# The 512x512 projections of a four-layer float32 attention kernel as seven half-size block products

## The chip, the cores and the metric

The kernel runs on one core of a Trainium2 chip. The metric is device time in microseconds (us), the median of several executions. All executions told here count as fast: none was over 1.5% above the fastest of its kernel. Executions of one kernel differ by up to 0.3% (2642.78 to 2650.27 us for the changed one), and a part of that spread turns out to have a cause of its own (see the experiment with filled waits). The granted clock is TensorE's clock as the profile records it, as a share of full speed.

TensorE is the matmul engine (PE in the profile, PEld for its weight loads), VectorE is DVE, ScalarE is ACT, SyncE is SP. SP's queue issues nearly all transfers (q1 on the page: 94.94 of 100.44 MB in the changed kernel). PSUM is the memory that TensorE writes its products to; the kernel uses it in pieces of 128x512 float32, called banks here. One float32 matmul leaves two records in the profile (a projection's 32 matmuls are 64 records). Line numbers (L326) differ between kernels.

## The reference, cut to what matters

Four layers follow one another on `x` of shape (4, 512, 32, 32), all in float32: four images of 512 channels and 1024 tokens.

```python
# layer 0: 8 heads of 64, softmax attention, residual
qkv = (xs @ Wp.T + bp).reshape(B, s, N_HEADS, 3 * D_K)
...
out = res @ Wo.T + bo + xs
# layer 1: linear attention: softplus features of 64, gated values, residual
# layer 2: layer norm over channels, one head of 512, residual
xn = (xf - mu) * jax.lax.rsqrt(var + EPS) * norm_w
qkv = jnp.einsum('bnc,dc->bnd', xn, w_qkv) + b_qkv
...
# layer 3: group norm (32 groups), 4 heads of 128, residual
qkv = conv1x1(group_norm(x, norm_w, norm_b), qkv_w, qkv_b)
...
return x + conv1x1(out, proj_w, proj_b)
```

Every projection is a 512x512 matrix times an image of 512x1024. There are four of them (q, k, v, output) per image in layers 0 and 3, and two in layer 2, where the kernel multiplies pairs of matrices into one beforehand (`wqk`, `wvo`).

## The kernel before

Everything goes by tiles of 128 partitions. `NC` is 4 (chunks of 128 channels), `TB` is 512 (half the tokens), `QT` is 4. Two pools of PSUM tiles matter: `acc` (two tiles of one bank) and `sc` (two tiles of two banks). A projection is a loop over token halves and output tiles, and its evictions (copies out of PSUM) alternate between VectorE and ScalarE:

```python
    def product(ps, lhs, rhs, cs=range(NC)):
        for c in cs:
            nc.tensor.matmul(
                ps, lhsT=lhs(c), rhs=rhs(c), start=(c == 0), stop=(c == NC - 1)
            )
...
    def project_qkv(w, bias, xb, first=False):
        ...
                for o in range(2 * NC):                  # q and k, by channels
                    ps = acc_tile()
                    product(
                        ps, lambda c: w[o // NC][:, c, bass.ts(o % NC, P)], lambda c: x[:, c, :]
                    )
                    slot()
                    evict(o, (q, k)[o // NC][tb][:, o % NC, :], ps, col(bias, o))
            for t in range(QT):                          # v, by tokens
                ps = acc_tile()
                product(ps, lambda c: x[:, c, bass.ts(t, P)], lambda c: w[2][:, c, :])
                slot()
                evict(t, v[tb][:, t, :], ps)
```

Work that is not on TensorE's path is cut into steps by generators and slipped between matmuls: each `slot()` runs one step of the first generator in `background` (linear attention of the image before, layer norm or group norm of the next), and `finish()` runs what is left of them at once. So how early background work is done depends on how many slots the stage ahead of it has. This will matter.

```python
    def slot():
        for p in pending:
            p[0] -= 1
        while pending and pending[0][0] <= 0:
            pending.pop(0)[1]()
        while background:
            if next(background[0], "end") != "end":
                break
            background.pop(0)
```

The layer norm of layer 2 has six steps for each half of the tokens, 12 in all; the last two of a half take the reciprocal of the deviation and write the normalized half (L592 and L595 in the prediction's lines). Layer 2's attention has 10 slots: two between score steps, and one for each of the four output chunks of both token halves. So the last two steps of the second half are left to `finish()` and run beside the next image's first products.

## Time and profile before

| | before |
|---|---|
| median of 3 executions | 2717.1 us (2716.29 to 2717.92) |
| span of the profiled execution | 2715.5 us |
| busy: TensorE, VectorE, ScalarE | 99%, 45%, 22% |
| moved by DMA | 32.17 MB |

The prediction shows the lines that say what bounds this kernel: TensorE, throughout. What TensorE waits for is very little, as the view of waits shows (engine, line, what it waited for: us in total, times, longest):

```profile
PE sc L289 <- ACT ptt L296: 7.4, 7, 2.9
PE sc L207 <- DMA wq<-in_wqkv: 5.6, 1, 5.6
PE sc L207 <- DVE q L371: 4.8, 1, 4.8
```

The first is at starts of attentions, where scores wait for exponentials; the second is the kernel's very first load; the third is its last projection. The largest two groups of projection matmuls on the page (columns: line, engine, operation, output and inputs, shape, count; then busy us and mean ns of one; then idle time ahead of them) have none:

```profile
L207 PE MATMUL po<-q,wo 128*128 128x512 f32 x480 | 211.6, 594 | 0.0
L207 PE MATMUL acc<-wv,x 128*128 128x512 f32 x256 | 115.9, 597 | 0.0
```

VectorE's float32 additions (`tensor_tensor`), on whose durations the prediction's costs rest, take 1217 ns for 128x1024 (L304) and 685 and 686 for 128x512 (L306, L371).

**A measure used below.** Waits in this view are only those where an instruction was released by another engine. To count all lost time, I took all of TensorE's records in order of start, and from each start-to-start time subtracted the pace of that record's shape (0.4289 us for 512 columns on the whole array, 0.2155 for 256, 0.111 for 128, 0.2145 for 512 columns on half the array, 0.07 for anything else). The paces are near the steps of the traces of before and after, whose medians are 0.429, 0.216 and 0.109 us for the first three shapes, and 0.430 for two records on half the array; the 0.07 is an assumption. The sum I call the *excess*. In the kernel before it is 89.4 us. Its absolute value depends on the paces chosen; differences between kernels hardly do.

### The profile page before, as it was taken

How to read it: one execution, taken by the hardware profiler on the slowest of the kernel's cores; microseconds unless marked ns; L12 is line 12 of the kernel's file. 1: busy time of each engine (PE TensorE's matmuls, PEld its weight loads, DVE VectorE, ACT ScalarE, POOL GpSimd, SP SyncE). 2: the span in 40 equal slices, each digit the busy share in tenths (PEclk: the TensorE clock that was granted, in tenths of full speed). 3: DMA queues.
4: the chain of work that ended last, by engine and by line, in shares of the span. 5: the costliest groups of instructions: out<-in, count | busy, mean ns of one | idle time of the engine just before them, and what ended most of it. 6: DMA issues, size and time to landing. Idle time of an engine off the chain costs nothing.

```text
span 2715.5 us, 17950 instructions
## 1 busy us (share of the span) xinstructions
PE 2690.0 (99%) x7490; PEld 1112.6 (41%) x7490; DVE 1232.7 (45%) x1359; ACT 602.5 (22%) x677; POOL 2.1 (0%) x12
## 2 busy tenths in 40 slices
PE   9999999999999999999999999999999999999998
PEld 4333433343334233444444444444444444444443
DVE  1466366636763877316144161321641651353154
ACT  0332143214321532111111111002310310220120
POOL 0000000000000000000000000000000000000000
PEclk9999999999999999999999999999999999999999
DMA  5000000000000000000000010000000000000000
GB/s 209 1 1 1 0 1 1 0 1 1 0 0 16 1 16 31 0 0 1 0 0 0 1 62 0 0 1 0 0 27 4 0 16 16 1 16 16 0 1 32
DMA packets 15448, 32.17 MB, mean 12 GB/s; under 512 B 1409, under 2 KB 1921, under 8 KB 15361
## 3 DMA queue, kind: packets, MB, share of 16 engines
q1 hardware_dynamic: 13056, 26.77, 2.7%
q10 hardware_dynamic: 2304, 4.20, 0.4%
q8 instruction: 60, 0.98, 0.2%
q14 instruction: 28, 0.22, 0.0%
HBM read 22.58 MB, written 8.39 MB: 11 GB/s over the span
## 4 chain that ended last, share of the span: by engine, by line
PE 96%; DVE 2%; ACT 1%; issue 0%; DMA 0%; SPq 0%; DVEq 0%; ACTq 0%
PE acc L207 32%; PE sc L289 25%; PE acc L322 16%; PE acc L337 8%; PE po L207 8%; PE den L358 1%; PE sc L207 1%; PE z L441 1%; PE den L353 1%; PE wval L543 1%; PE kx L488 1%; PE xtr L479 1%; PE kv L207 1%; PE lnsum L571 0%; DVE sum L304 0%
## 5 line engine op out<-in xcount | busy, mean ns | idle before, releaser
L296 ACT ACTIVATE ptt<-sc 128x1024 f32<-128x1024 f32 x416 | 412.0, 1022 | 843.3 <-PE sc L289 748.4
L289 PE MATMUL sc<-q,k 64*128 64x512 f32 (+1 forms) x1536 | 486.9, 610 | 7.4 <-ACT ptt L296 7.4
L322 PE MATMUL acc<-ptt,v 128*64 128x512 f32 (+1 forms) x1536 | 476.6, 600 | 0.0
L304 DVE TENSOR_TENSOR sum<-sum,ptt 128x1024 f32<-128x1024 f32 x272 | 330.9, 1217 | 218.5 <-ACT ptt L296 207.7
L289 PEld LDWEIGHTS sc<-q,k 64*128 64x128 f32 (+1 forms) x1536 | 184.5, 187 | 292.2 <-issue 204.0
L360 DVE RECIPROCAL r<-den 128x512 f32<-128x512 f32 x72 | 241.6, 3356 | 121.4 <-PE den L358 119.9
L322 PEld LDWEIGHTS acc<-ptt,v 128*64 128x64 f32 (+1 forms) x1536 | 159.7, 154 | 292.6 <-issue 289.0
L337 PE MATMUL acc<-ptt,v 128*128 128x512 f32 x512 | 223.4, 592 | 0.0
L289 PE MATMUL sc<-q,ln 128*128 128x512 f32 x512 | 221.1, 592 | 0.0
L207 PE MATMUL po<-q,wo 128*128 128x512 f32 x480 | 211.6, 594 | 0.0
L300 DVE TENSOR_TENSOR sum<-ptt 128x1024 f32<-128x1024 f32 x72 | 87.8, 1219 | 172.6 <-ACT ptt L296 171.9
L337 PEld LDWEIGHTS acc<-ptt,v 128*128 128x128 f32 x512 | 97.2, 190 | 122.0 <-issue 121.3
L289 PEld LDWEIGHTS sc<-q,ln 128*128 128x128 f32 x512 | 97.2, 190 | 122.0 <-issue 122.0
L220 DVE COPY v<-acc 128x512 f32<-128x512 f32 x48 | 33.2, 692 | 243.0 <-PE acc L207 243.0
L207 PEld LDWEIGHTS po<-q,wo 128*128 128x128 f32 x480 | 90.4, 190 | 118.0 <-issue 115.7
L386 DVE SCALAR_TENSOR_TENSOR x<-po,cs,x 128x512 f32<-128x512 f32 x60 | 45.1, 751 | 176.8 <-PE po L207 176.8
L207 PE MATMUL acc<-wv,x 128*128 128x512 f32 x256 | 115.9, 597 | 0.0
L207 PE MATMUL acc<-wvo,ln 128*128 128x512 f32 x256 | 113.1, 594 | 0.0
L207 PE MATMUL acc<-ln,wqk 128*128 128x512 f32 x256 | 112.2, 593 | 0.0
L207 PE MATMUL acc<-gn,wq 128*128 128x512 f32 x256 | 111.7, 592 | 0.0
L207 PE MATMUL acc<-gn,wk 128*128 128x512 f32 x256 | 111.2, 592 | 0.0
L207 PE MATMUL acc<-wv,gn 128*128 128x512 f32 x256 | 111.2, 592 | 0.0
(147 smaller groups left out, 1703.4 us busy)
## 6 DMA issues: line engine op xcount, KB each, us to landing
x<-in_x SPq DMA_DIRECT2D x3, 2048.0 KB, 20.4
out<-x SPq DMA_DIRECT2D x16, 256.0 KB, 2.0
out<-x ACTq DMA_DIRECT2D x16, 256.0 KB, 2.0
wo<-in_wo SPq DMA_DIRECT2D x3, 1024.0 KB, 5.5
wv<-in_wqkv SPq DMA_DIRECT2D x2, 1024.0 KB, 6.7
x<-in_x SPq DMA_DIRECT2D x4, 256.0 KB, 4.9
wq<-in_wqkv SPq DMA_DIRECT2D x4, 256.0 KB, 5.1
wk<-in_wqkv SPq DMA_DIRECT2D x4, 256.0 KB, 5.6
```

What stands on the lines that cost most here:

```text
L207: nc.tensor.matmul(ps, lhsT=lhs(c), rhs=rhs(c), start=(c == 0), stop=(c == NC - 1))
L220: nc.vector.tensor_copy(dst, ps)
L289: nc.tensor.matmul(ps[:, half, :], lhsT=s.k[key // QT][p0:p1, c, bass.ts(key % QT, P)], rhs=s.q[qb][p0:p1, c, :], start=(n == 0), stop=(n ...
L296: nc.scalar.activation(pt, ps, AF.Exp, scale=s.scale)
L300: nc.vector.tensor_tensor(t, s.pts[i - 1], pt, ALU.add)
L304: nc.vector.tensor_tensor(t, t, pt, ALU.add)
L322: nc.tensor.matmul(ps[p0:p1, :], lhsT=s.v[key // QT][:, key % QT, g * P + p0 : g * P + p1], rhs=pt[:, half, :], start=(key == 0), stop=(ke ...
L337: nc.tensor.matmul(ps, lhsT=s.v[key // QT][:, key % QT, bass.ts(n, P)], rhs=parts[key // 2][:, key % 2, :], start=(key == 0), stop=(key == ...
L353: nc.tensor.matmul(ps[half * s.hd : (half + 1) * s.hd, :], lhsT=ones[:, : s.hd], rhs=t[:, half, :], start=True, stop=True,)
L358: nc.tensor.matmul(ps, lhsT=ones, rhs=t[:, 0, :], start=True, stop=True)
L360: nc.vector.reciprocal(r, ps)
L386: nc.vector.scalar_tensor_tensor(xv, ps, s.eb[:, o : o + 1], xv, ALU.add, ALU.add)
```

## The change

The intent: split weights, inputs and outputs into 2x2 blocks of half size and compute the product with seven block products in place of eight, at the price of additions: 4 for the weights, 4 for the inputs, 7 for the outputs. Weights no longer stay in SBUF: they and their sums (kept in DRAM) are loaded anew for each image. The output projection moves from the middle of the attention to behind the next image's q. The order of products within a call, and which PSUM bank each goes to, is the table `SEVEN`: the last four products accumulate on a bank that has already been read once.

```diff
+    SEVEN = [
+        (1, 0, "put", (0, 0)), (2, 1, "add", (0, 0)), (7, 2, "put", (1, 1)), (6, 0, "put", (1, 0)),
+        (4, 2, "add", (1, 0)), (5, 0, "add", (1, 1)), (3, 0, "put", (0, 1)),
+    ]
...
+    def right(xb, tiles, over=False):
+        b11, b21 = xb[0][:, :HC, :], xb[0][:, HC:, :]
+        b12, b22 = xb[1][:, :HC, :], xb[1][:, HC:, :]
...
+        tt(t3, b22, b12, ALU.subtract)
+        tt(t1, b12, b11, ALU.subtract)
+        tt(t2, b22, t1, ALU.subtract)
+        tt(t4, b21, t2, ALU.subtract)
+        return {1: b11, 2: b21, 3: b22, 4: t4, 5: t1, 6: t2, 7: t3}
...
+    def two_by_sevens(factors, n, put, add):
+        banks = []
+        for _ in range(2):
+            pair_of = sc_tile()
+            banks.append([acc_tile()[:, :n], pair_of[:, 0, :n], pair_of[:, 1, :n]])
+        for i, bank, do, block_of in SEVEN:
+            for which in range(2):
+                ps = banks[which][bank]
+                for j in range(HC):
+                    lhs, rhs = factors(which, i, j)
+                    first = i in (1, 2, 7)
+                    nc.tensor.matmul(
+                        ps, lhsT=lhs, rhs=rhs, start=first and j == 0, stop=(j == HC - 1),
+                        skip_group_check=not first,
+                    )
+                (put if do == "put" else add)(which, block_of, ps)
+            slot()
...
+    def project_qkv(loads, bias, xb, before):
+        x = right(xb, [pt_tile] * 4)
+        q = [block("q") for _ in range(NTB)]
+        channels_first(loads.take("q"), x, q, bias=lambda o: col(bias, o))
+        if before is not None:
+            loads.start("k")
+            project_out(before, loads.take("o"))
+            loads.start("v")
...
+        k = [block("k") for _ in range(NTB)]
+        channels_first(loads.take("k"), x, k, bias=lambda o: col(bias, NC + o))
+        v = [block("v") for _ in range(NTB)]
+        tokens_first(loads.take("v"), x, v)
+        return q, k, v
...
+    def prepare():
+        for part in "qkvo":
+            if part == "o":
+                w = load("wo", d["wo3"])
+            else:
+                w = load("w", d["wqkv3"], "qkv".index(part))
+            for _ in range(3):
+                yield
+            keep_sums(f"{part}3", w)
+            yield
+        eb3.append(column_sums(w, "bqkv3", 2, "bo3"))
+        loads.start("q", "k")
+        yield
...
         else:
-            wo3 = load("wo", d["wo3"])
-            w3 = [load(n, d["wqkv3"], i) for i, n in enumerate(("wq", "wk", "wv"))]
             start_norm(group_norm, 0, "gn0")
+            background.append(prepare())
         Attention(b, q, xn, v, 1, None, eb).run()
         finish()
```

`put` is an eviction on ScalarE, `add` an addition from PSUM into the output on VectorE. `prepare`, which makes the sums of layer 3's weights and starts its first loads, runs in the background of layer 2's last attention.

More of the change, by code (lines that the diff above doesn't have):

```diff
@@ L67, in conv_fast @@
     PSUM = bass.MemoryType.PSUM
+    dram = ctx.enter_context(tc.tile_pool(name="dram", bufs=1, space=bass.MemoryType.DRAM))
     ps_acc = ctx.enter_context(tc.tile_pool(name="ps_acc", bufs=2, space=PSUM))
@@ L113, in conv_fast @@
         nc.sync.dma_start(xs[b], xin[b])
-    wv1 = load("wv1", d["wv1"])
-    w1 = block("w1")
-    wqk1 = w1[:, 0, :].rearrange("p (c o) -> p c o", c=NC)
-    nc.sync.dma_start(wqk1, by_chunk(d["wqk1"]))
-    bv1 = w1[:, 1, :]
-    nc.sync.dma_start(bv1, d["bv1"].partition_broadcast(P))
     bqk1 = const.tile([P, 2], F32, name="bqk1")
@@ L220, in evict, with first_qkv @@
             nc.vector.tensor_copy(dst, ps)
-    def project_qkv(w, bias, xb, first=False):
+    def first_qkv(w, bias, xb):
         q, k, v = [], [], []
@@ L233, in project_qkv @@
             v.append(block("v"))
-            if first and tb == 0:
+            if tb == 0:
                 banks = [s[:, i, :] for s in (sc_tile(), sc_tile()) for i in range(2)]
@@ L259, in project_qkv, with weight_parts, weight_sums @@
         return q, k, v
+    SEVEN = [
+        (1, 0, "put", (0, 0)), (2, 1, "add", (0, 0)), (7, 2, "put", (1, 1)), (6, 0, "put", (1, 0)),
+        (4, 2, "add", (1, 0)), (5, 0, "add", (1, 1)), (3, 0, "put", (0, 1)),
+    ]
+    HC = NC // 2
+    HO = C // 2
+    def weight_parts(w):
+        return w.rearrange("p (h j) (m n) -> p h j m n", h=2, m=2)
+    def weight_sums(w, name):
+        t = block(name)
+        s = t.rearrange("p c t -> p (c t)").rearrange("p (i j n) -> p i j n", i=4, j=HC)
+        a = weight_parts(w)
+        tt = nc.vector.tensor_tensor
+        tt(s[:, 0], a[:, 0, :, 1, :], a[:, 1, :, 1, :], ALU.add)
+        tt(s[:, 1], s[:, 0], a[:, 0, :, 0, :], ALU.subtract)
+        tt(s[:, 2], a[:, 0, :, 0, :], a[:, 0, :, 1, :], ALU.subtract)
+        tt(s[:, 3], a[:, 1, :, 0, :], s[:, 1], ALU.subtract)
+        return t
@@ new lines, in left @@
+    def left(w, sums):
+        a = weight_parts(w)
+        s = sums.rearrange("p c t -> p (c t)").rearrange("p (i j n) -> p i j n", i=4, j=HC)
+        return {
+            1: a[:, 0, :, 0, :], 2: a[:, 1, :, 0, :], 4: a[:, 1, :, 1, :],
+            5: s[:, 0], 6: s[:, 1], 7: s[:, 2], 3: s[:, 3],
+        }
+    def right(xb, tiles, over=False):
+        b11, b21 = xb[0][:, :HC, :], xb[0][:, HC:, :]
+        b12, b22 = xb[1][:, :HC, :], xb[1][:, HC:, :]
+        tt = nc.vector.tensor_tensor
+        t3, t2, t4 = (tiles[i]() for i in range(3))
+        t1 = b12 if over else tiles[3]()
+        tt(t3, b22, b12, ALU.subtract)
[3 more added lines that the diff above has]
+        return {1: b11, 2: b21, 3: b22, 4: t4, 5: t1, 6: t2, 7: t3}
@@ new lines, in pt_tile @@
+    def pt_tile(name="ptt"):
+        return work.tile([P, 2, TB], F32, tag="pt", bufs=5, name=name)
+    def two_by_sevens(factors, n, put, add):
[15 more added lines that the diff above has]
+            slot()
@@ new lines, in channels_first, with factors, first, more @@
+    def channels_first(a, b, out, put=None, bias=None):
+        def factors(which, i, j):
+            return a[i][:, j, bass.ts(which, P)], b[i][:, j, :]
+        def first(which, at, ps):
+            o = 2 * at[0] + which
+            if bias is None:
+                nc.scalar.copy(out[at[1]][:, o, :], ps)
+            else:
+                nc.scalar.activation(out[at[1]][:, o, :], ps, AF.Identity, bias=bias(o))
+        def more(which, at, ps):
+            c = out[at[1]][:, 2 * at[0] + which, :]
+            nc.vector.tensor_tensor(c, ps, c, ALU.add)
+        two_by_sevens(factors, TB, put or first, more)
@@ new lines, in tokens_first, with factors, at_block, put @@
+    def tokens_first(a, b, out):
+        for t0 in range(0, QT, 2):
+            def factors(which, i, j):
+                return b[i][:, j, bass.ts(t0 + which, P)], a[i][:, j, :]
+            def at_block(which, at):
+                return out[at[1]][:, t0 + which, bass.ts(at[0], HO)]
+            def put(which, at, ps):
+                nc.scalar.copy(at_block(which, at), ps)
+            def add(which, at, ps):
+                c = at_block(which, at)
+                nc.vector.tensor_tensor(c, ps, c, ALU.add)
+            two_by_sevens(factors, HO, put, add)
@@ new lines, in conv_fast, with keep_sums, load_left, __init__ @@
+    sums_in_dram = {}
+    def keep_sums(key, w):
+        t = weight_sums(w, "wsum")
+        kept = dram.tile([P, NC, TB], F32, tag=key, name="kept")
+        nc.sync.dma_start(kept, t)
+        sums_in_dram[key] = kept
+    def load_left(key, src, part=0):
+        w = load("w", src, part)
+        s = block("ws")
+        nc.sync.dma_start(s, sums_in_dram[key])
+        return left(w, s)
+    class Loads:
+        def __init__(s, layer):
+            s.layer, s.ready = layer, {}
+        def start(s, *parts):
+            for part in parts:
+                if part == "o":
+                    s.ready[part] = load_left(f"o{s.layer}", d[f"wo{s.layer}"])
+                else:
+                    i = "qkv".index(part)
+                    s.ready[part] = load_left(f"{part}{s.layer}", d[f"wqkv{s.layer}"], i)
+        def take(s, part):
+            return s.ready.pop(part)
@@ new lines, in project_out, with put, add, factors @@
+    def project_out(att, a):
+        b = right(att.q, [lambda: pair("t3"), lambda: pair("t2"), pt_tile], over=True)
+        def put(which, at, ps):
+            o = 2 * at[0] + which
+            att.add_to_x(at[1], o, ps, done=(at == (0, 1)))
+        def add(which, at, ps):
+            o = 2 * at[0] + which
+            xv = xs[att.b][:, o, bass.ts(at[1], TB)]
+            nc.vector.tensor_tensor(xv, ps, xv, ALU.add)
+            att.store_x(at[1], o)
+        def factors(which, i, j):
+            return a[i][:, j, bass.ts(which, P)], b[i][:, j, :]
+        two_by_sevens(factors, TB, put, add)
@@ new lines, in project_qkv @@
+    def project_qkv(loads, bias, xb, before):
[6 more added lines that the diff above has]
+            loads.start("v")
+        else:
+            loads.start("v")
+        if before is not None and before.then is not None:
+            background.append(before.then())
+        k = [block("k") for _ in range(NTB)]
[3 more added lines that the diff above has]
+        return q, k, v
@@ L261, in conv_fast, with __init__ @@
     class Attention:
-        def __init__(s, b, q, k, v, heads, wo, eb, store=False, last=False):
+        def __init__(s, b, q, k, v, heads, wo, eb, store=False, last=False, then=None):
             s.b, s.q, s.k, s.v, s.wo, s.eb = b, q, k, v, wo, eb
-            s.store, s.last = store, last
+            s.store, s.last, s.then = store, last, then
             s.hd = C // heads
@@ L294, in scores @@
                     )
-            pt = work.tile([P, 2, TB], F32, tag="pt", bufs=5, name="ptt")
+            pt = pt_tile()
             nc.scalar.activation(pt, ps, AF.Exp, scale=s.scale)
@@ L371, in normalize @@
             nc.vector.tensor_tensor(s.q[qb][:, g, :], s.accs.pop((qb, g)), r, ALU.mult)
-            if g == s.groups - 1 and not (s.last and qb == NTB - 1):
+            if s.last and g == s.groups - 1 and qb < NTB - 1:
                 later(3, lambda: s.project_out(qb))
@@ L382, in out_product, with add_to_x, store_x @@
             product(ps, lambda c: s.wo[:, c, bass.ts(o, P)], lambda c: s.q[qb][:, c, :], cs)
-        def add_to_x(s, qb, o, ps):
+        def add_to_x(s, qb, o, ps, done=True):
             xv = xs[s.b][:, o, bass.ts(qb, TB)]
             nc.vector.scalar_tensor_tensor(xv, ps, s.eb[:, o : o + 1], xv, ALU.add, ALU.add)
+            if done:
+                s.store_x(qb, o)
+        def store_x(s, qb, o):
             if s.store:
-                (nc.scalar if o % 2 else nc.sync).dma_start(xout[s.b, :, o, bass.ts(qb, TB)], xv)
+                (nc.scalar if o % 2 else nc.sync).dma_start(
+                    xout[s.b, :, o, bass.ts(qb, TB)], xs[s.b][:, o, bass.ts(qb, TB)]
+                )
         def run(s):
@@ L651, in idle @@
             yield
-    eb = None
+    att = None
+    loads = Loads(0)
     for b in range(B):
         xb = [xs[b][:, :, bass.ts(tb, TB)] for tb in range(NTB)]
-        if b > 0:
-            background.append(idle(3))
-            background.append(linear_attention(b - 1))
-        q, k, v = project_qkv(w0, "bqkv0", xb, first=(b == 0))
         if b == 0:
+            for key, w in zip(("q0", "k0", "v0", "o0"), w0 + [wo]):
+                keep_sums(key, w)
+            q, k, v = first_qkv(w0, "bqkv0", xb)
             eb = column_sums(wo, "bqkv0", 2, "bo0")
+            wv1 = load("wv1", d["wv1"])
+            w1 = block("w1")
+            wqk1 = w1[:, 0, :].rearrange("p (c o) -> p c o", c=NC)
+            nc.sync.dma_start(wqk1, by_chunk(d["wqk1"]))
+            bv1 = w1[:, 1, :]
+            nc.sync.dma_start(bv1, d["bv1"].partition_broadcast(P))
+        else:
+            q, k, v = project_qkv(loads, "bqkv0", xb, att)
         if b == B - 1:
@@ L665, in conv_fast @@
             rawk = load("rawk", d["wraw2"], 1)
-        Attention(b, q, k, v, 8, wo, eb).run()
+            rawq = load("rawq", d["wraw2"], 0)
+        else:
+            loads.start("q", "o")
+        att = Attention(b, q, k, v, 8, None, eb, then=lambda b=b: linear_attention(b))
+        att.run()
+    loads.start("o")
     finish()
-    rawq = load("rawq", d["wraw2"], 0)
-    rawv = load("rawv", d["wraw2"], 2)
-    wo = load("wo", d["wo2"])
-    background.append(linear_attention(B - 1))
     def fold(lhs, rhs, name):
@@ L688, in conv_fast @@
     u = column_sums(rawk, "bqkv2", 0)
+    flush()
+    rawv = load("rawv", d["wraw2"], 2)
+    wo = load("wo", d["wo2"])
+    project_out(att, loads.take("o"))
+    background.append(att.then())
+    wqk = left(wqk, weight_sums(wqk, "wqks"))
     wvo = fold(rawv, wo, "wvo")
     eb = column_sums(wo, "bqkv2", 2, "bo2")
+    wvo = left(wvo, weight_sums(wvo, "wvos"))
+    loads = Loads(3)
+    eb3 = []
+    def prepare():
+        for part in "qkvo":
+            if part == "o":
+                w = load("wo", d["wo3"])
+            else:
+                w = load("w", d["wqkv3"], "qkv".index(part))
[6 more added lines that the diff above has]
+        yield
     for b in range(B):
         xn = norms.pop(f"ln{b}")
-        q, v = [], []
-        for tb in range(NTB):
-            q.append(block("q"))
-            v.append(block("v"))
-            for o in range(NC):
-                ps = acc_tile()
-                product(ps, lambda c: wqk[:, c, bass.ts(o, P)], lambda c: xn[tb][:, c, :])
-                slot()
-                evict(o, q[tb][:, o, :], ps, u[:, o : o + 1])
-            for t in range(QT):
-                ps = acc_tile()
-                product(ps, lambda c: xn[tb][:, c, bass.ts(t, P)], lambda c: wvo[:, c, :])
-                slot()
-                evict(t, v[tb][:, t, :], ps)
+        x = right(xn, [pt_tile] * 4)
+        q = [block("q") for _ in range(NTB)]
+        channels_first(wqk, x, q, bias=lambda o: u[:, o : o + 1])
+        v = [block("v") for _ in range(NTB)]
+        tokens_first(wvo, x, v)
         if b + 1 < B:
@@ L710, in conv_fast @@
         else:
-            wo3 = load("wo", d["wo3"])
-            w3 = [load(n, d["wqkv3"], i) for i, n in enumerate(("wq", "wk", "wv"))]
             start_norm(group_norm, 0, "gn0")
+            background.append(prepare())
         Attention(b, q, xn, v, 1, None, eb).run()
         finish()
-    eb = column_sums(wo3, "bqkv3", 2, "bo3")
+    att = None
     for b in range(B):
-        q, k, v = project_qkv(w3, "bqkv3", norms.pop(f"gn{b}"))
-        if b + 1 < B:
+        last = b == B - 1
+        q, k, v = project_qkv(loads, "bqkv3", norms.pop(f"gn{b}"), att)
+        if last:
+            wo = load("wo", d["wo3"])
+        else:
             start_norm(group_norm, b + 1, f"gn{b + 1}")
-        Attention(b, q, k, v, 4, wo3, eb, store=True, last=(b == B - 1)).run()
+            loads.start("q", "o")
+        att = Attention(b, q, k, v, 4, wo if last else None, eb3[0], store=True, last=last)
+        att.run()
         finish()
```

## The prediction

> **What bounds the kernel now.** I read the page's busy times first, then its slices, then the chain that ended last.
>
> ```profile
> span 2715.5 us, 17950 instructions
> PE 2690.0 (99%) x7490; PEld 1112.6 (41%) x7490; DVE 1232.7 (45%) x1359; ACT 602.5 (22%) x677; POOL 2.1 (0%) x12
> ...
> PE   9999999999999999999999999999999999999998
> ...
> DVE  1466366636763877316144161321641651353154
> ...
> PE 96%; DVE 2%; ACT 1%; issue 0%; DMA 0%; SPq 0%; DVEq 0%; ACTq 0%
> PE acc L207 32%; PE sc L289 25%; PE acc L322 16%; PE acc L337 8%; PE po L207 8%; PE den L358 1%; PE sc L207 1%; PE z L441 1%; PE den L353 1%; PE wval L543 1%; PE kx L488 1%; PE xtr L479 1%; PE kv L207 1%; PE lnsum L571 0%; DVE sum L304 0%
> ```
>
> TensorE is busy in every slice and is 96% of the chain. Line 207 is the helper that every 512x512 projection goes through, and holds 40% of the chain (acc and po). A busy PE need not be a PE at its pace, so I took the pace from the timeline of two projections of the last layer, and from a burst of narrow matmuls in layer 1:
>
> ```profile
> 2516.94 13.90 PE L207 MATMUL acc<-gn,wq 128*128 128x512 f32 x32
> 2530.68 13.90 PE L207 MATMUL acc<-gn,wk 128*128 128x512 f32 x32
> ...
> 311.97 1.05 PE L507 MATMUL kxt<-halves,kx 128*128 128x128 f32 x8
> ```
>
> From start to start, 32 records take 13.74 us: 0.4293 us each, with no gap. The program has half as many matmuls, so one float32 matmul is two records, 0.859 us for 512 columns. The narrow ones: the last of the 8 lasts 0.275 us (that line's median), so 7 steps take 0.775 us, 0.111 us each. A weight load is listed as 0.19 us there too, and yet the step is 0.111: loads overlap each other as well as matmuls. So matmuls of 256 columns, between the two, should run at half the 512-column step, near 0.216 us, and not be held by their weight loads.
>
> [...]
> - [...] Only multiplications with TensorE count here; the additions that replace them cost TensorE nothing.
> - [...] 1217 ns for 1024 elements (line 304), 685 to 690 for 512.
> - [...] bank 0 is read after products 1, 6, 5 and 3 and accumulated on in between. Only waits, no extra instructions; no part of the trace before does it.
>
> **What the change removes.** A projection of one image (512x512 weights by 1024 tokens) is now 4 x 4 x 2 = 32 matmuls, 64 records, 27.5 us. Seven half-size products are 7 x 2 output tiles x 2 chunks = 28 matmuls of 512 columns (56 records, 24.0 us), or, where tokens come first, 56 of 256 columns (112 records x 0.2158, about 24.2 us). The eighth that falls away is 8 x 0.4293 = 3.43 us.
>
> How many projections change, from the diff: layer 0 images 1 to 3 q, k, v and all four outputs, 13; layer 2 q and v of four images, 8; layer 3 q, k, v of four and the output of three, 15. In all 36 (25 by channels, 11 by tokens); the first image's q, k, v and the last output stay. So TensorE loses 36 x 3.43 = 123.6 us, and gets back 11 x 0.13 = 1.5 for halved columns.
>
> **What it adds.** On VectorE, all from the durations above:
> - Input sums: 4 subtractions of 128x1024, 4.9 us, for 11 inputs (q, k and v share one) and 7 outputs: 88 us.
> - Adds into C: 6 of 512 (0.69 us) per channel call, 12 of 256 (estimate 0.42, from the slope between 512 and 1024) per token call. Against the evictions that VectorE now makes (4 a projection, or 8 in an output), that is about +1.1 us for each of 18 q/k, +2.3 for 11 v, +4.1 for 7 outputs: 74 us.
> - Weight sums, 4 x 0.69 us for 10 matrices: 28 us.
>
> Together +190 us, so VectorE goes to about 1420 of 2600 us, 55%: off the path as a whole. ScalarE gets the plain evictions, +3 to 5 us a projection, and has room at 22%.
>
> Transfers: 28 loads of 2 MB (weights and sums) and 8 MB of sums written. The start of the trace moves about 400 GB/s and single 1 MB weight loads land in 5.0 to 7.8 us, so a pair needs some 11 us. q and o are loaded over a whole attention stage (110 us and more); k waits for old k and v blocks, but is used only two products later, 48 us; v gets q's blocks, 48 us before its use. Hidden.
>
> **What can come onto the path.** Four places.
>
> (a) Within a call, product 3 accumulates in the bank of product 5, and must wait for VectorE's add of 5. With two tiles interleaved there is one tile's product in between: 4 x 0.429 = 1.72 us. An eviction starts about 0.21 us after the next product does (VectorE's q eviction at 2520.58; the product that starts at 2516.94 ends 8 steps later, at 2520.37), takes 0.69, and TensorE starts about 0.11 us after a release (scores at 360.85 after an exponential that ends at 360.74): 1.0 of 1.72. By tokens it is 0.21 + 0.42 + 0.11 = 0.74 of 0.86. It fits, but any 1.2 us instruction ahead of the add on VectorE stalls TensorE up to 0.5 to 1.1 us. That happens where VectorE has other work: beside linear attention, and while the next sums are made. Estimate 1.5 us for each of the six handovers between images in layers 0 and 3, and 2 us for each of three linear attentions beside projections: 15 us.
>
> (b) Layer 2 is tighter, since seven-product order wants both token halves at once:
>
> ```profile
> 1625.09 13.90 PE L207 MATMUL acc<-ln,wqk 128*128 128x512 f32 x32
> ...
> 1626.01 3.35 DVE L592 RECIPROCAL rstd<-rstd 128x512 f32<-128x512 f32 x1
> ...
> 1629.85 2.73 DVE L595 SCALAR_TENSOR_TENSOR ln<-ln,cols,rstd 128x512 f32<-128x512 f32 x4
> ```
>
> The normalized second half is ready at 1632.6, 7.5 us after projections start; today it is first read 27 us after. Products 1 and 2 need only the first half and last 6.9 us; product 7 needs one subtraction more (1.2 us), at 8.7. So 1.9 us of stall, in three of four images: 6 us.
>
> (c) At a handover, both accumulators must be free before product 1 of the second tile, and the last group's is freed only after its denominators, 3.4 us reciprocal and multiplication: in layer 3 the last value matmul is through at 2460.9 and that multiplication at 2467.0. Product 1 of the first tile and product 2 of both (5.2 us) can go first. Under 1 us, counted in (a).
>
> (d) The first and the middle stage (sums of first weights, output of image 3 between two foldings, layer 3's sums made in the background): VectorE is idle from 24 to 31 us, DRAM traffic there ends at 40. Estimate 3 us.
>
> Sum: 2717.1 - 123.6 + 1.5 + 15 + 6 + 3 = 2619; I state 2617, since a schedule can move instructions past a stall.
>
> **Rivals.**
> 1. *VectorE takes over in layer 0.* In its attention it has 108 busy of 158 us (the stretch from 92 to 250), and without the output product in mid attention that stretch shrinks by 13.7 us for TensorE but only 3 for VectorE. If linear attention also slid there (it now starts two products later), it would exceed 85%. It has about 20 steps, and k and v offer 21 slots, so I think it still ends before. If not, some 10 us in each of three images: 2650.
> 2. *The bank chain stalls at every call*, because evictions are queued behind input sums: 47 two-tile calls (25 + 22) at 1 us would be 47 us: 2650. For it: slack by tokens is only 0.12 us. Against: VectorE has 8.0 busy of 67.9 us in layer 3's projections now (2035 to 2103).
> 3. *Narrow matmuls are bound by weight loads* at 0.3 us: 11 x 112 x 0.085 = 105 us more, 2720, the gain gone. The 0.111 us step speaks against it, though only in bursts of 8.
> 4. *No stalls:* 2717.1 - 122 = 2595.
>
> **Range and chances.** The removal is sure arithmetic; the uncertainty is all stalls, from nearly none (2597) to rivals 1 or 2 (2650). The 2% line lies at 2662.8, so stalls would have to reach 68 us. Faster by over 2%: 0.93; within: 0.06; slower: 0.01.
>
> **What would show it.** Right: PE busy near 2570, in the seven-product group 0.43 us a record of 512 columns and 0.216 of 256; idle of PE before these products, released by VectorE, 15 to 30 us in all; VectorE near 1420; no wait of PE on a load over 1 us after the start. Wrong: token products above 0.25 us a record; PE idle in layer 0's attention behind VectorE; a wait for sums from DRAM at the start of layer 3 or at k.

## The result, and the profile after

| | before | after |
|---|---|---|
| median | 2717.22 us (2716.29 to 2717.92, 4 runs) | 2649.31 us (2642.78 to 2650.27, 4 runs) |
| ratio | | 0.9745 (95%: 0.9728 to 0.9762): faster |
| span of the profiled execution | 2715.5 us | 2641.1 us |
| excess over pace | 89.4 us | 137.3 us |
| moved by DMA | 32.17 MB | 100.44 MB |

Ratios are the mean time of one kernel's fast runs over that of the other's in the same rounds, so not quite the ratio of the medians. The gain is 68 us where 100 were forecast. The time lies inside the stated range, at its very edge.

The page of the changed kernel, in the parts that the prediction shows of before (busy times, VectorE's slices, the chain that ended last):

```profile
span 2641.1 us, 19557 instructions
...
PE 2584.7 (98%) x7818; PEld 1174.1 (44%) x7818; DVE 1410.6 (53%) x1637; ACT 690.1 (26%) x881; POOL 2.1 (0%) x12
...
DVE  2486477646864887426345153252762563365254
...
PE 92%; DVE 4%; ACT 2%; issue 1%; DMA 0%; SPq 0%; DVEq 0%; ACTq 0%
PE sc L470 25%; PE acc L326 18%; PE acc L503 17%; PE sc L326 12%; PE acc L518 8%; PE acc L202 3%; PE den L539 1%; PE sc L202 1%; PE z L628 1%; PE den L534 1%; PE wval L730 1%; PE kx L675 1%; DVE sum L485 1%; PE xtr L666 1%; PE po L202 1%
```

TensorE lost 105 us of busy time and is still the bound. VectorE gained 178 us, to 1410.6, and has no slice above 8 tenths. But TensorE's share of the chain fell from 96% to 92%, and VectorE's doubled: some of the path now runs through VectorE. The projections are lines 326 (30% of the chain; the first image's and the folded ones are still line 202).

**The pace is as forecast.** The timeline of the last image's v in layer 3, by tokens (start us, duration us, engine, line, operation and count):

```profile
2464.49 1.89 PE L326 MATMUL acc<-ws,ptt 128*128 128x256 f32 x8
2466.22 1.89 PE L326 MATMUL sc<-w,ptt 128*128 128x256 f32 x8
2467.95 1.89 PE L326 MATMUL acc<-ws,ptt 128*128 128x256 f32 x8
```

Eight records take 1.73 us, 0.216 us each. In numbers for the whole: the span fell by 74.4 us and the excess rose by 47.9, so the work at pace fell by 122.3, against 123.6 - 1.5 = 122.1 in the prediction. The whole miss is in the excess.

**Where the excess came from.** The view of TensorE's waits, without the three lines that answer to those of before (7.1, 5.3 and 4.8 us) and the ones below 1.6 us:

```profile
PE sc L326 <- DVE ptt L303: 11.2, 3, 3.8
PE acc L326 <- DMA w<-in_wqkv: 7.5, 1, 7.5
...
PE sc L326 <- DVE q L348: 4.2, 3, 1.4
PE acc L326 <- ACT v L363: 3.4, 4, 0.9
PE sc L326 <- DVE v L367: 2.6, 3, 0.9
```

Two lines make 18.7 of these 28.9 us. The first is product 7 at the start of images 1 to 3 in layer 2. The timeline of the last of them:

```profile
1591.01 3.35 DVE L779 RECIPROCAL rstd<-rstd 128x512 f32<-128x512 f32 x1
...
1595.51 0.69 DVE L348 TENSOR_TENSOR q<-sc,q 128x512 f32<-128x512 f32 x1 [1.15 <-PE sc L326]
...
1596.12 2.73 DVE L782 SCALAR_TENSOR_TENSOR ln<-ln,cols,rstd 128x512 f32<-128x512 f32 x4
1598.76 0.68 DVE L348 TENSOR_TENSOR q<-sc,q 128x512 f32<-128x512 f32 x1
1599.36 1.22 DVE L303 TENSOR_TENSOR ptt<-ln 128x1024 f32<-128x1024 f32 x1
...
1600.64 3.70 PE L326 MATMUL sc<-ptt,wqks 128*128 128x512 f32 x8 [3.52 <-DVE ptt L303]
```

VectorE worked here in the order of its queue. After the reciprocal, which ends at 1594.36, it sits 1.15 us waiting for product 2 of the first tile, because that tile's add (1595.51) stands ahead of the normalization; then come the four normalizing instructions, then the second tile's add, and only then the difference `t3` (L303) that product 7 reads. The adds cost 1.4 us and the wait 1.15. TensorE, from the start-to-start times, loses 3.68 us here and 3.99 twice before.

The second line is layer 3's first weight load. VectorE and the DMA queue of SP, in the timeline of that start:

```profile
1752.91 1.20 SPq L100 DMA_DIRECT2D w<-in_wqkv  x1
...
1761.97 0.68 DVE L283 TENSOR_TENSOR wsum<-wo,wsum 128x512 f32<-128x512 f32 x1
1762.55 2.05 PE L326 MATMUL acc<-gn,w 128*128 128x512 f32 x2 [7.51 <-DMA w<-in_wqkv]
...
1762.68 0.34 SPq L377 DMA_DIRECT2D kept<-wsum  x1
1763.12 0.38 SPq L383 DMA_DIRECT2D ws<-kept  x1
```

The load of q's weights was issued at 1752.91, 2 us before TensorE wanted them, and TensorE ran on at 1762.55. The sums (`ws`) were loaded later still: they stand in SP's queue behind the store of the output matrix's sums, which were finished at 1762.65. `prepare` needs 17 slots and comes after group norm, which takes 8 of the attention's 10. So most of `prepare` is run by `finish()`, at the end, all at once.

The smaller lines are in layer 0. The handover of images, at q of image 1:

```profile
222.40 3.35 DVE L541 RECIPROCAL r<-den 128x512 f32<-128x512 f32 x1
...
225.67 0.63 DVE L348 TENSOR_TENSOR q<-sc,q 128x512 f32<-128x512 f32 x1
...
226.35 1.98 PE L326 MATMUL sc<-ptt,ws 128*128 128x512 f32 x4 [1.38 <-DVE q L348]
```

The add of product 2 stands behind a reciprocal of the last attention's denominators, and product 7 of the same tile starts only after the add. It costs 1.55 us of TensorE's time in each of three images. The `v` lines are evictions that stand behind linear attention's softplus, on ScalarE (1.10 us, three times) and on VectorE (1.04, three times). Last, there are steps that are 0.07 to 0.15 us too long, 0.10 on average: between two records of one shape they are 124 in this kernel and 72 before. The recorded texts call them restarts after a wait, but the profile records a release within 0.3 us before only 23 of the 124 and 4 of the 72, so what delays the others is not shown.

### The profile page after: what moved, and what is told of

Same layout as the page of the kernel before. It is cut to its first block, busy times and chain, and to the rows that moved or that the text cites. A ratio compares the mean times of both kernels' runs of the same rounds, so it can differ in the third digit from the quotient of the medians.

```text
span 2641.1 us, 19557 instructions
## 1 busy us (share of the span) xinstructions
PE 2584.7 (98%) x7818; PEld 1174.1 (44%) x7818; DVE 1410.6 (53%) x1637; ACT 690.1 (26%) x881; POOL 2.1 (0%) x12
## 2 busy tenths in 40 slices
DMA packets 35953, 100.44 MB, mean 38 GB/s; under 512 B 2448, under 2 KB 2960, under 8 KB 31248
## 4 chain that ended last, share of the span: by engine, by line
PE 92%; DVE 4%; ACT 2%; issue 1%; DMA 0%; SPq 0%; DVEq 0%; ACTq 0%
PE sc L470 25%; PE acc L326 18%; PE acc L503 17%; PE sc L326 12%; PE acc L518 8%; PE acc L202 3%; PE den L539 1%; PE sc L202 1%; PE z L628 1%; PE den L534 1%; PE wval L730 1%; PE kx L675 1%; DVE sum L485 1%; PE xtr L666 1%; PE po L202 1%
## 5 line engine op out<-in xcount | busy, mean ns | idle before, releaser
L367 DVE TENSOR_TENSOR v<-sc,v 128x256 f32<-128x256 f32 x88 | 37.3, 424 | 144.8 <-PE sc L326 143.1
L326 PE MATMUL acc<-ptt,ws 128*128 128x512 f32 x224 | 102.5, 595 | 0.0
L363 ACT COPY v<-acc 128x256 f32<-128x256 f32 x132 | 48.7, 372 | 148.1 <-PE acc L326 148.1
L344 ACT ACTIVATE k<-acc,cols 128x512 f32<-128x512 f32 x42 | 28.9, 687 | 215.2 <-PE acc L326 215.2
L567 DVE SCALAR_TENSOR_TENSOR x<-acc,cs,x 128x512 f32<-128x512 f32 x74 | 55.4, 749 | 51.9 <-PE acc L326 51.3
L326 PE MATMUL sc<-ptt,w 128*128 128x512 f32 x168 | 76.6, 594 | 0.0
L344 ACT ACTIVATE q<-acc,cols 128x512 f32<-128x512 f32 x42 | 28.9, 687 | 175.7 <-PE acc L326 175.7
L326 PEld LDWEIGHTS acc<-ptt,ws 128*128 128x128 f32 x224 | 42.1, 190 | 55.2 <-issue 50.7
L348 DVE TENSOR_TENSOR q<-sc,q 128x512 f32<-128x512 f32 x44 | 29.9, 679 | 68.1 <-PE sc L326 68.1
L348 DVE TENSOR_TENSOR k<-sc,k 128x512 f32<-128x512 f32 x28 | 19.4, 691 | 81.4 <-PE sc L326 81.4
```

The lines of the kernel that those rows point to most:

```text
L326: nc.tensor.matmul(ps, lhsT=lhs, rhs=rhs, start=first and j == 0, stop=(j == HC - 1), skip_group_check=not first,)
L344: nc.scalar.activation(out[at[1]][:, o, :], ps, AF.Identity, bias=bias(o))
L348: nc.vector.tensor_tensor(c, ps, c, ALU.add)
L567: nc.vector.scalar_tensor_tensor(xv, ps, s.eb[:, o : o + 1], xv, ALU.add, ALU.add)
```

## The experiments

Twelve runs, all correct. The first four ran on one chip and the other eight on a second; the kernel before took 2717.85 us in the first round, and 2717.55 and 2716.84 in the two on the second chip. The main theory: the missing 32 us are the two long waits, and both come from how early background work is done, not from the seven products. The rival: they come from the call's own structure (chain of banks, two-bank tiles, narrow token products). The two moves below settle the 30 us that they win; the 24 us of excess over the kernel before that they leave stay with the rival, in part open.

**after_again**, the changed kernel unchanged, as a measure.

> The changed kernel again, as the measure for the other three. In its profile TensorE loses 48 us more in steps longer than their pace than the kernel before does. Theory A (named waits): 13.5 us of it at the starts of three images of layer 2, 10.6 us at the start of layer 3, the rest in layer 0 and in restarts of 0.1 us. After each wait of some 4 us TensorE runs steps of 0.85 in place of 0.43 us in some executions and not in others, which is why executions differ: expect 2642 to 2651, clock 0.991 to 0.995. Rival B (the loss is spread over all 47 two-tile calls): the same time, but the same loss of about 1 us in every call.

Measured: 2649.2 us (2648.55 to 2649.33), 0.9746 of before's 2717.85. The excess of this profiled execution is 143.1 us, so the 2642.78 of the first was a lucky one (137.3).

**norm_early.** Layer 2's layer norm gets more slots, so that it is through before the next image starts:

```diff
                 s.add_to_x(qb, n, ps)
                 slot()
+                if s.b + 1 < B:
+                    slot()
...
-                if not s.one or i % s.per:
+                if not s.one or i % s.per or s.b + 1 < B:
                     slot()
```

> The layer norm of the next image runs two steps where it ran one in layer 2's attention, so it is done before the projections start. Theory A: the three waits of product 7 for its input sum (3.99, 3.99 and 3.68 us) go, and the slow steps after them: 12 to 17 us less than the changed kernel of the same round, clock up by 0.002 to 0.003. Rival B: at most 4 us less. Rival C (VectorE is too full in layer 2, the earlier norm only moves the wait into the attention): TensorE waits in layer 2's attention instead, under 4 us gained.

Measured: 2633.02 us (2630.77 to 2633.79), ratio 0.9688 (0.9672 to 0.9704): 16.2 us less than after_again. In the timeline of image 1's start the second group is product 7, and it follows the group before without a gap:

```profile
1256.88 3.60 PE L326 MATMUL sc<-ln,wqk 128*128 128x512 f32 x8
...
1260.32 3.60 PE L326 MATMUL sc<-ptt,wqks 128*128 128x512 f32 x8
```

All three waits are gone from the view of waits, and nothing has come in their place. They summed to 11.7 us (3.99, 3.99, 3.68), so 4.5 us more were won than were waited; the filled waits below say why.

**prep_early.** `prepare` moves to the background of layer 0's first attention, and layer 3's first loads are started at the start of layer 2's last attention:

```diff
+        elif b == 0:
+            background.append(prepare())
...
         att.run()
+        if b == 0:
+            finish()
...
             start_norm(group_norm, 0, "gn0")
-            background.append(prepare())
+            loads.start("q", "k")
```

> Layer 3's sums are made during the first image of layer 0 in place of the last of layer 2; its first q and k weights are loaded in layer 2's last attention. Theory A: the wait of 7.7 us on the load at the start of layer 3 goes with its slow steps: 9 to 12 us less. Rival C: VectorE (11 us of sums more beside layer 0's first attention, where it is 80% full) holds TensorE there, and the gain is under 5 us.

Measured: 2635.24 us (2632.47 to 2638.82), ratio 0.9692 (0.9676 to 0.9708): 14.0 us less in the median, a little more than expected. The wait on the load is gone, and layer 0 shows no new one. Between the two profiled executions the difference is only 10.5 us (2649.33 to 2638.82), which is what the wait accounts for; the other three executions had a higher granted clock (0.995 to 0.997 against 0.993).

**all_three.** Both moves, and product 6 ahead of product 7 everywhere but in layer 2's q (the edit is shown under swap).

> Both, and product 6 before product 7 everywhere but in layer 2's q, so that the add of product 2 has twice the time before TensorE writes the same two-bank tile. Theory A: 22 to 28 us from the two, 3 to 8 us from the order: about 2613 to 2622, executions within 2 us of each other, clock 0.998 or more. Rival B: 2640 or more, and the spread stays.

Measured: 2618.45 us (2616.69 to 2618.76), ratio 0.9632 (0.9616 to 0.9648). The sum of the first two gains, 30.2 us, gives 2619.0 already, so the order was worth nearly nothing here, against expectation. The granted clock is 0.997 in every execution.

**swap.** Only the order. Product 6 needs the bank of product 1, long evicted by ScalarE, where product 7 waits for VectorE's add of product 2, as the handover's timeline shows:

```diff
+    SWAPPED = SEVEN[:2] + [SEVEN[3], SEVEN[2]] + SEVEN[4:]
...
-        for i, bank, do, block_of in SEVEN:
+        for i, bank, do, block_of in order or SWAPPED:
...
-        channels_first(wqk, x, q, bias=lambda o: u[:, o : o + 1])
+        channels_first(wqk, x, q, bias=lambda o: u[:, o : o + 1], order=SEVEN)
```

> The changed kernel with product 6 before product 7, except in layer 2's q. Theory D (in the two-bank tile, product 7 waits for VectorE's add of product 2, though that lies in the other bank): the wait of 1.55 us in layer 0's q (3 times) and of 1.04 us in its v (3 times) shrink or go, about 3 to 8 us less than the changed kernel (2649). Rival (these waits belong to a full VectorE and only move to the next instruction that needs it, as the three changes together suggested, which gave 30.8 us where the first two alone gave 16.2 and 14.0): within 2 us of 2649, and a wait on VectorE of 0.7 to 1.3 us beside each of these places.

Measured: 2645.1 us (2643.93 to 2648.84), ratio 0.9738 (0.9721 to 0.9754), which overlaps that of after_again. The wait at the handover shrank, and others grew, in linear attention and in v:

```profile
PE nd L721 <- DVE z L612: 3.3, 3, 1.1
...
PE sc L327 <- ACT v L364: 2.3, 1, 2.3
PE sc L327 <- DVE q L349: 1.6, 3, 0.5
```

The handover went from 4.2 to 1.6 us, linear attention (nd) from 1.5 to 3.3, and the first image of layer 2 gained a wait of 2.3. The verdict is open between nothing and some 5 us (4.1 under after_again, 5.5 under after_third on the same chip).

**own_tile.** In the old order, product 2 of q in layers 0 and 3 gets a tile of its own, in place of half of a two-bank tile. If the handover's wait came only from two products sharing a tile, it should go.

```diff
-            banks.append([acc_tile()[:, :n], pair_of[:, 0, :n], pair_of[:, 1, :n]])
+            second = tr_tile("second")[:, :n] if apart else pair_of[:, 0, :n]
+            banks.append([acc_tile()[:, :n], second, pair_of[:, 1, :n]])
```

> The changed kernel with product 2 of layer 0's and 3's q in a tile of its own, not in one two-bank tile with product 7. Theory D: product 7's wait on the add of product 2 (1.55 us, three times in layer 0) is gone from the profile, with nothing in its place: 3 to 5 us less than 2649. Rival: product 7 still starts only when that add has ended, or waits for another VectorE instruction of the same stretch: within 2 us.

Measured: 2647.3 us (2646.74 to 2648.65), ratio 0.9743 (0.9727 to 0.9759): the same. Product 7 of the first tile no longer waits: at image 1 it starts at 222.63, before the add of product 2 (226.06). But a wait of the same size stands at a new place, product 2 of the second tile, which needs the first one's bank to be free:

```profile
PE second L327 <- DVE q L349: 4.2, 3, 1.4
```

The pool of this tile has only two, and the denominators that the reciprocal reads hold the other. So in both layouts TensorE waits for the same add, late behind VectorE's reciprocal. That sharing costs nothing is not shown: a layout with a free bank was not run.

**tokens_plain.** All eleven v projections go back to plain products of 512 columns, with everything else as changed.

```diff
-        tokens_first(loads.take("v"), x, v)
+        tokens_plain(loads.take("v"), xb, v)
...
-        tokens_first(wvo, x, v)
+        tokens_plain(wvo, xn, v)
```

> The changed kernel with all eleven v projections as plain products of 512 columns, as before the change. Theory A: each costs 27.5 in place of 24.1 us of TensorE, 11 x 3.3 = 36 us more, against waits of 256-column products of about 15 us that go: 2665 to 2678. Rival (halved columns are held up, so that the token products bring little or nothing): 2649 or less.

Measured: 2661.03 us (2659.71 to 2662.1), ratio 0.979 (0.9774 to 0.9806), 11.8 us above after_again; expected were 16 or more. The token products win, but a third of what they take off: 11 x 3.43 - 1.5 = 36 us of work at pace. The excess tells where the rest stays: it is 119.6 us here against 143.1, so 23.5 us of waits and longer steps come with the token products, and 36 - 23.5 = 12.5, near the difference of the two profiled spans (2660.4 - 2647.6 = 12.8).

**lin_own.** The two moves, own tiles, and two steps of linear attention in each slot of layer 0's k, to be done with softplus before v:

```diff
                 (put if do == "put" else add)(which, block_of, ps)
             slot()
+            if twice[0]:
+                slot()
```

> Early layer norm, early sums for layer 3 and own tiles for product 2, and two steps of linear attention for one beside layer 0's k, so that its second softplus falls beside k, where a product gives 1.7 us of room, and not beside v, where it gives 0.86. Theory A: 30 us from the first two, 3 to 5 from the own tiles, up to 6 from the last (the waits of 1.1 and 1.0 us in each of three images): 2607 to 2616. Rival (VectorE is full beside k then): 2618 or more, with new waits in k.

Measured: 2622.94 us (2622.58 to 2623.11), ratio 0.9651 (0.9635 to 0.9667). That is a miss, and 4.5 us slower than all_three. Waits in v remain (behind VectorE, 5.8 us in six), and q's 4.2 too. Moving work within a full stage moved the wait. Which of the two additions makes it 3.5 us slower than the two moves alone (two_moved, 2619.44) was not separated.

**filled.** The last theory concerns the size of the two long waits. Records just after a wait of 3.5 us or more often run at half pace: in the first profile they step at 0.853 us in place of 0.429 after the waits of 3.83 us at 1264.25 and 4.79 at 2629.20. To test that it is idleness and not the place, TensorE was given matmuls of no use during the waits:

```diff
+    def filling(n):
+        ps = tr_tile("fill")
+        for _ in range(n):
+            nc.tensor.matmul(ps, lhsT=ones, rhs=xs[0][:, 0, :TB], start=True, stop=True)
...
         for i, bank, do, block_of in SEVEN:
+            if i == 1 and fill[0]:
+                filling(fill[0])       # 8, first q tile of layer 3
+            if i == 7 and fill[1]:
+                filling(fill[1])       # 4, first q tile of images 1 to 3 in layer 2
```

> The new kernel with matmuls of no use in its four longest new waits: 4 matmuls of 512 columns (8 records, 3.43 us) ahead of product 7 of the first q tile in layer 2 for images 1 to 3, and 8 (16 records, 6.9 us) ahead of product 1 of the first q tile of layer 3. They read data that has long been there, and their result is used by nothing. The end of each wait is set by VectorE or a load and doesn't move; only the idle time of TensorE is gone. Theory (a wait of 3.5 us or more makes TensorE run its next records at half pace in most executions): the waits for t3 and for w shrink to under 1 us each, there are 6 or fewer 512-column records with an excess of 0.35 to 0.5 us after the first 20 us, the granted clock goes from 0.991-0.993 to 0.995 or more, and the time falls by 2 to 6 us, to 2643 to 2647, with a spread of under 3 us. Rival 1 (the slow records come from the place, from fresh tiles or from VectorE's and the queues' work there, and not from idleness): slow records and time as in the new kernel, 2648 to 2650. Rival 2 (the filling itself delays: its last record ends after the release): up to 1 us slower at each place, 2650 to 2653.

> The new kernel unchanged, as the measure for the filled waits on the same chip: 2647 to 2650, with single executions down to 2643, granted clock 0.991 to 0.995.

The unchanged kernel on the same chip (after_third) took 2650.63 us (2647.99 to 2650.72), at a clock of 0.991 to 0.993. Its timeline at the starts of images 1 and 2 in layer 2:

```profile
1264.99 5.40 PE L326 MATMUL sc<-ptt,wqks 128*128 128x512 f32 x8 [3.83 <-DVE ptt L303]
...
1434.19 6.24 PE L326 MATMUL sc<-ptt,wqks 128*128 128x512 f32 x8 [3.83 <-DVE ptt L303]
```

With filled waits, the start of image 1:

```profile
1264.42 3.70 PE L337 MATMUL sc<-ptt,wqks 128*128 128x512 f32 x8 [0.40 <-DVE ptt L303]
```

The same eight records last 5.40 and 6.24 us after a wait and 3.70 when TensorE was kept busy: 1.7 and 2.5 us, which is four and six records at 0.86 instead of 0.43. Over layer 2's three starts, records of 512 columns that took 0.3 to 0.55 us too long are 15 in after_third, 13 in after_again, 4 in the first profile, and none in filled. The granted clock agrees. The view by windows, of image 2's start in after_third and then in filled (stretch, its length, busy us and records of PE, PEld, DVE, ACT and POOL, granted clock, DMA share, GB/s):

```profile
1432.60:1439.30 6.70, 5.11 (x6) 2.16 (x7) 5.63 (x6) 0.69 (x1) 0.00 (x0) 0.50 0.00 0
...
1428.00:1445.00 17.00, 16.60 (x40) 7.17 (x39) 10.04 (x13) 2.75 (x4) 0.00 (x0) 1.00 0.00 0
```

Not every such wait ended so: of the three starts, one had half clock in the first profile and all three in after_again, and after these waits of 3.7 to 4.0 us none to six records of 512 columns were slow. A wait of 2.9 us was enough in the kernel before: TensorE waits for exponentials up to 932.4, and the clock is 0.50 from 932.8 to 936.2.

The time was a miss: 2649.54 us (2649.3 to 2650.47) where 2643 to 2647 were expected. The trace shows why: in layer 3 the fill ran at 1765.14, after the wait of 7.5 us, because the schedule had put it behind the first matmul of product 1. There it only delayed, by 16 x 0.4289 = 6.9 us. Without that, an estimate, the time would be 2642.7, 8 us under the unchanged kernel, of which 15 x 0.42 = 6.3 are the slow records. The theory is shown for layer 2; the filling of layer 3's wait was not tested, and there the clock stayed at 0.50 (from 1758.4 to 1768.7).

**two_moved** and **all_three_again**, on the same chip, for the order of the products once more.

> Only the two moves together, layer 2's layer norm earlier and layer 3's sums made in layer 0, with the products in the old order. If the two gains add and the order of products 6 and 7 is worth nothing, 2649.2 - 16.2 - 14.0 = 2619, the same as all three within 1.5 us. If the order is worth the 3 to 8 us first expected of it, this is 2621 to 2626. If the order costs something where the other waits are gone, 2614 to 2617.

> All three moves again, to compare on the same chip with the two: 2618.5 within 1.5 us.

Measured: 2619.44 us (2618.11 to 2621.41), ratio 0.9643 (0.963 to 0.9656), for the two moves, and 2617.42 us (2616.48 to 2619.51), ratio 0.9636 (0.9623 to 0.9649), with the order. The two gains add: against after_third it is 31.2 us. The order is worth some 2 us at best, within the overlap of both ranges. The fastest kernel is all_three, some 100 us under the kernel before and 31 under the change as it was.

## Why the prediction was right or wrong

The direction, the class and the mechanism were right: TensorE bound, work at pace down by 122.3 us, narrow matmuls at half the step, VectorE at 1410.6 busy where 1420 was forecast, and 18.7 us of waits before these products that VectorE ended (11.2 + 4.2 + 2.6 + 0.7), where 15 to 30 were named. PE busy is 2584.7, not near 2570. The size was off by 32 us (2649.3 against 2617), and the terms that were mis-sized are the waits:

| term | predicted | shown by the runs |
|---|---|---|
| matmuls removed, halved columns | -122.1 | -122.3 |
| (a), (c) bank chain, handovers, linear attention | 15 | 23.9 (excess of two_moved, 113.3, less that of before, 89.4) |
| (b) layer 2's starts | 6 | 16.2 (norm_early): waits of 11.7, the rest slow records |
| (d) start and middle, with layer 3's sums | 3 | 14.0 (prep_early): waits of 7.7 and 1.0, the rest slow records, some of them elsewhere |

The last two differ from the forecast by 21 us and the first of the three waits by 9: together 30 of the 32. The two rows of moved work are medians of runs that took the cause away, so they are shown. The share of slow records in (d) is inferred.

- **Step (b) failed in its detail.** The forecast had `t3` ready 1.9 us after product 2 is through: second half normalized, then one subtraction. It left out that VectorE ran in the order of its queue (1594.36 to 1600.6 in the timeline above), and that the two adds of product 2 stand in that queue, one ahead of the normalization and one behind it. VectorE so waited for TensorE (1.15 us), and TensorE then for VectorE. Moreover the clock fell to 0.50 after these waits of 3.7 to 4.0 us, at all three starts in after_again and after_third, which the forecast did not count.
- **Step (d) was only an estimate of 3**, from VectorE's idle time at the start. It looked at whether the sums fit, not at when the slots would let them be made; and "Hidden", said of the loads that are started an attention ahead, does not hold for layer 3's first ones, which start at `prepare`'s last step. The prediction named "a wait for sums from DRAM at the start of layer 3" as a sign of being wrong: the wait came, though on the weights' load and not on the sums'. "No wait of PE on a load over 1 us" was wrong, at 7.5 us.
- **Step (a) has the right stages and cause, but the wrong link, and lacks the small waits.** It put the stall at product 3, behind the add of product 5. Only one product 3 waits for an add (0.87 us, layer 2's first image). The others are product 7 behind the add of product 2 (1.55 in q, 1.04 in v, three times each), and product 1 of a token call behind ScalarE's eviction (1.10, three times). That the sum for layer 0 still fits the forecast is partly luck. Handovers cost 3 x 1.55 us in layer 0 (forecast: six of 1.5, layers 0 and 3), linear attention 3 x 2.14 beside v and 3.3 in the fourth image (forecast: 3 x 2), with three small ones of 0.26 that is 15.1 us. The remaining 9 were not forecast; 52 more of the steps that are 0.1 us too long account for about 5, and their cause is open. The rest is not settled. The partial sums read inside an accumulation group gave correct results in every run, and took no extra matmuls: the 7818 records of the page are 7490 - 36 x 64 + 25 x 56 + 11 x 112.
- **Rival 1**, VectorE takes over in layer 0: not so, no wait on VectorE lies in its attention. **Rival 2**, a stall of 1 us at every call: no; there are about 15 waits over 0.6 us in line 326, in 47 calls, and a call has about two steps that are 0.1 us too long. **Rival 3**, weight loads bind narrow matmuls: no, 0.216 us. **Rival 4**, no stalls: no.

That the two moves alone give 2619.4, close to the forecast 2617, is partly luck: there (b) and (d) are gone while (a) is 24, which happens to be the forecast's sum of all three.

## What to carry to other kernels

The arithmetic saving on the bounding engine arrived in full here (122.3 us of work at pace, where 122.1 were forecast), but each new dependence on another engine's queue must be checked in that queue's order, and not by summing durations: at the start of an image in layer 2, an add that waited 1.15 us for TensorE held up all that stood behind it on VectorE, and TensorE then lost 3.68 us. Background work that runs by free slots should be counted slot by slot against the stage that has to hide it. Waits of TensorE of 2.9 us and more mostly went with half clock here (six of the eight in the profiles of before and after, the first load left out), and so cost more than their length. Two separate small moves here, neither of which touched the seven products, brought back 31 of the missing 32 us.
